# Depthwise 7x7 stage of a fused two-layer kernel: per-channel scalars laid out from diagonals made earlier, and the last step's output interleaved in two halves

## The chip, the cores and the metric

The kernel runs on one core of one Trainium2 chip. A core has the matrix engine TensorE (PE in the profile, its weight loads PEld), VectorE (DVE), ScalarE (ACT) and GpSimd (POOL); SyncE (SP) issues DMA transfers, and so do the queues of ACT and POOL. Each engine executes its own instructions in order; between engines there are semaphores. The metric is the device time of one launch in microseconds, lower is better. Times of a profiled execution are given from the start of its span.

## The reference, cut to what matters

The input is one image of 384 channels, 192 x 192, in fp32. Layer 0 is a group norm, a 1x1 convolution to 1152 channels with 2x2 max pooling, a 3x3 depthwise convolution, channel attention with four top-k softmaxes, a GELU, 2x2 repetition, a projection, and a residual sum. Layer 1 is what the change touches:

```python
def _dwconv(x, w, stride, pad):       # one 7x7 filter for each channel, pad 3
    C = x.shape[1]
    return lax.conv_general_dilated(x, w, window_strides=(stride, stride),
        padding=[(pad, pad), (pad, pad)], dimension_numbers=('NCHW', 'OIHW', 'NCHW'),
        feature_group_count=C)
def _L1_conv_ref(x, weight):
    w_sym = (weight + rot90(weight, 1) + rot90(weight, 2) + rot90(weight, 3)) * 0.25
    return _dwconv(x, w_sym, STRIDE, PAD)
...
x = x + _L1_conv_ref(_gn(x), L1_conv_weight)   # _gn: 32 groups of 12 channels
```

The group norm of layer 1 is `(x - mean) / std` with a mean and a standard deviation for each channel's group, so each channel has three scalars: mean, std and rstd = 1/std.

## The kernel before, in words

The kernel first reads x for the statistics of the first norm, then runs the 1x1 convolution of q and k, the attention, and v with the projection. The sum of layer 0 goes to a DRAM tile `sd` in the layout that the 7x7 stage reads; the banded filter matrices of the 7x7 stage go to `wt` and `wh` in DRAM. This takes up to about 2231 us of the span.

The **7x7 stage** follows. It is a loop of 48 steps, n = 0 to 47, each of CB = 8 channels. For a step, four transfers on ACT's queue load `w` and `h` (filter matrices) and `main` and `aux` (the image, 128 partitions of CP = 4 column strips times TR = 32 rows, and a halo). Each of these has three buffers, and the loads for step n + 2 are issued at the start of step n. Before a step can run, `borders` (POOL, lines 1332 to 1359) writes the mean into the image's border, from `mm` and `mb`; `rest` and `columns` (ACT, lines 1371, 1195, 1196) copy parts of the image and of the filters; and `middle` (DVE, line 1271) adds the residual, std times a permuted identity `eye`, to the middle of the filter matrices, from `sb`.

A step handles its channels in four pairs, q = 0 to 3. For a pair, `sums` makes one PSUM tile `pc` of two banks: for each channel three matmuls (line 1419), two on `main` with `w`, one on `aux` with `h`; an fp32 matmul is two passes in the profile. The tile is then scaled by rstd (from `rb`) into `apart`, in four pieces of 32 partitions: on DVE for q = 0 and 2 (line 1439), on ACT for q = 1 and 3 (line 1437). After q = 1 the loop runs `middle`, `rest` and `columns` of the next step. The pool `pc` has four buffers; the tiles `al` below come from it too.

`apart` holds the four columns of a strip group apart from each other. `spread` (POOL, line 1381) interleaves them into `res` with two copies of 128 x 1152, and SP issues four transfers of 288 KB of it to the output (line 1385), one for each 32 partitions. `spread` of step n - 1 is called in step n behind `borders` of step n + 1, and for step 47 after the loop. `res` has two buffers, `apart` three.

The scalars `mb`, `sb`, `rb` and `mm` lie along the free dimension, 384 channels wide, equal on all partitions. They are made in three tiles of 128 channels. `along` does it: DVE scales the identity by the scalar of each partition into a diagonal `al_dg` (line 1283), PE multiplies ones by it into an `al` tile (line 1284), and DVE copies the tile out (line 1285); `masked` (DVE, line 1289) then makes `mm` of `mb`. The first tile is made ahead of the loop. The other two, kt = 1 and 2, are made at the end of steps 2 and 3:

```python
            if 1 < n < KT + 1:
                done = [along(d, v, n - 1) for d, v in ((mb, mean1), (sb, std1), (rb, rstd1))]
                for d in done:
                    d()
                masked(n - 1)
```

The calls in `keep(...)` stay in the order of the program on their engine, so for this stage the order of the text is the order of each queue.

Of the kernel before, what the change touches and what calls it, by code (L numbers as in the profile page):

```python
# [8 lines left out]
F32 = mybir.dt.float32  # L9
# [4 lines left out]
P = 128  # L14
C = 384
KT = C // P
# [35 lines left out]
TR = 32  # L52
NT = HW // TR
CP = 4
NJ = HW // CP
# [23 lines left out]
def conv_preact_d2(  # L79
# [17 lines left out]
    nc = tc.nc  # L97
# [16 lines left out]
    ident = const.tile([P, P], F32, name="ident")  # L114
    make_identity(nc, ident)
    ones = const.tile([P, P], F32, name="ones")
# [62 lines left out]
    def over_groups(pool, src, n, name):  # L179

        ps = pool.tile([P, KT, n], F32, name=name)
        for jt in range(KT):
            kts = [kt for kt in range(KT) if abs(jt - kt) < 2]
            for kt in kts:
                nc.tensor.matmul(
                    ps[:, jt, :],
                    gsel[:, kt, jt * P : (jt + 1) * P],
                    src[:, kt, :],
                    start=(kt == kts[0]),
                    stop=(kt == kts[-1]),  # L190
                )
        return ps
# [7 lines left out]
    def about(mv, mid, name):  # L200

        d = const.tile([P, KT, 2], F32, name=f"about_{name}")
        nc.vector.tensor_tensor(d[:, :, 0], mv[:, :, 0], mid, ALU.subtract)
        nc.vector.tensor_tensor(d[:, :, 1], d[:, :, 0], d[:, :, 0], ALU.mult)
        nc.vector.tensor_tensor(d[:, :, 1], d[:, :, 1], mv[:, :, 1], ALU.add)
        return d
# [82 lines left out]
    keep = tc.keep_in_program_order  # L289
    with tc.tile_pool(name="stp", bufs=1) as stp, tc.tile_pool(name="xsp", bufs=5) as xsp:  # L290
# [29 lines left out]
        def total(name, n, terms):  # L320

            ps = ptr.tile([P, C], F32, name=name, tag="tr")
            for i, (lhs, rhs) in enumerate(terms):
                keep(
                    nc.tensor.matmul(
                        ps[:, 0:n], lhs, rhs, start=(i == 0), stop=(i == len(terms) - 1)
                    )
                )
            return ps[:, 0:n]

        def sel(kt, jt):
            return gsel[:, kt, jt * P : (jt + 1) * P]
# [15 lines left out]
        def both(kt, most, mid):  # L348

            last = moments(aggregate(kt, 0, NX, "last"), mid, f"{kt}_last")  # L350
            nc.vector.scalar_tensor_tensor(most, last, NX / NB, most, ALU.mult, ALU.add)
            return most
# [20 lines left out]
        for b in reversed(range(NB)):  # L373
            if b == NX - 1:
# [7 lines left out]
                for k, i in ((0, 0), (1, 1), (KT, 2)):  # L382
                    ps = total(f"gs_mid0_{k}", 1, terms[i])
# [54 lines left out]
        kt = TWO  # L438
        mid = mids[:, kt : kt + 1]
        for b in [*range(NB - 2, NX, -2), NX, *reversed(range(NX))]:  # L440
            n = 2 if b > NX else 1
            if b == NX - 1:
                most = aggregate(kt, NX, NB, "most")
                ps = total(
                    "gs_mid0_2", 1,
                    [(sel(1, 2), means[1]), (shared[:, P:], me), (whole, most[:, 0:1])],
                )
# [12 lines left out]
        d = both(kt, dm, mid)  # L460
        ps = total("gs0_2", 2, [(sel(1, 2), ds[1]), (shared[:, P:], de), (whole, d)])
# [89 lines left out]
    with ExitStack() as bx:  # L551
# [55 lines left out]
        with tc.issue_after(loaded):  # L607
            for kt in range(KT):
                cs = slice(kt * P, (kt + 1) * P)
# [535 lines left out]
    with ExitStack() as ex_:  # L1145
# [5 lines left out]
        wide = ex_.enter_context(tc.tile_pool(name="wide", bufs=1))  # L1151
# [5 lines left out]
        outp = ex_.enter_context(tc.tile_pool(name="outp", bufs=2))  # L1157
# [7 lines left out]
        steps = C // CB  # L1165
# [25 lines left out]
        def columns(n):  # L1191

            k = 2 * TR
            w, h = ws[n]
            keep(nc.scalar.copy(h[0:TR, :, 0 : 2 * TR], w[k : k + TR, :, 6 * TR :]))
            keep(nc.scalar.copy(h[REST:P, :, 0:TR], w[k : k + TR, :, 7 * TR :]))
# [46 lines left out]
        mean1 = const.tile([P, KT], F32, name="mean1")  # L1243
        rstd1 = const.tile([P, KT], F32, name="rstd1")
# [6 lines left out]
        with tc.tile_pool(name="gps1", bufs=1, space=PSUM) as gps:  # L1251
            ps = over_groups(gps, mid1.unsqueeze(2), 1, "gs_mid1")
# [3 lines left out]
            ps = over_groups(gps, about(mv1, gmid, "1"), 2, "gs1")  # L1256
            norm_of(ps, gmid, mean1, rstd1, "1")
        std1 = const.tile([P, KT], F32, name="std1")
        mb, sb, rb = [wide.tile([P, C], F32, name=name) for name in ("mb", "sb", "rb")]
        mm = wide.tile([P, C, 5], F32, name="mm")  # L1260

        def tiled(kt):
            return slice(kt * P, (kt + 1) * P)
# [12 lines left out]

        pc = ex_.enter_context(tc.tile_pool(name="pc", bufs=4, space=PSUM))

        def along(dst, src, kt):

            ps = pc.tile([P, 2, 512], F32, name=f"al{kt}", tag="pc")
            dg = wide.tile([P, P], F32, name=f"al_dg{kt}", tag="al_dg", bufs=3)
            keep(nc.vector.tensor_scalar_mul(dg, ident, src[:, kt : kt + 1]))
            keep(nc.tensor.matmul(ps[:, 0, 0:P], ones, dg, start=True, stop=True))
            return lambda: keep(nc.vector.tensor_copy(dst[:, tiled(kt)], ps[:, 0, 0:P]))

        def masked(kt):
            keep(
                nc.vector.tensor_tensor(
                    mm[:, tiled(kt), :],  # L1290
                    mb[:, tiled(kt)].unsqueeze(2).to_broadcast([P, P, 5]),
                    mask.unsqueeze(1).to_broadcast([P, P, 5]),
                    ALU.mult,
                )
            )
# [78 lines left out]
                )  # L1374
            )

        def spread(n, apart):

            res = outp.tile([P, 2, NT * NJ, CP], F32, name=f"res{n}", tag="res")
            for k in range(2):  # L1380
                keep(nc.gpsimd.tensor_copy(res[:, k], apart[:, :, k].rearrange("p e n -> p n e")))  # L1381
            for q in range(CP):
                c = n * CB + 2 * q
                keep(
                    nc.sync.dma_start(
                        out[c : c + 2].rearrange("c (t r) w -> r (c t) w", t=NT),
                        res[q * TR : (q + 1) * TR].rearrange("p c (t j) e -> p (c t) (j e)", t=NT),
                    )
                )

        columns(0)
        borders(0)
        rest(0)
        last = None
        for n in range(steps):
            if n + 2 < steps:
                ws[n + 2] = load_w(n + 2), load_h(n + 2)
                mains[n + 2] = load_main(n + 2), load_aux(n + 2)
            if n + 1 < steps:
                borders(n + 1)  # L1400
            if last is not None:
                spread(n - 1, last)
            (w, h), (main, aux) = ws.pop(n), mains.pop(n)
            apart = outp.tile([P, CP, 2, NT * NJ], F32, name=f"apart{n}", tag="apart", bufs=3)
            ahead = {}

            def sums(q, steps):

                if q not in ahead:
                    ahead[q] = pc.tile([P, 2, 512], F32, name=f"pc{n}_{q}", tag="pc")  # L1410
                for k in range(2):
                    i = 2 * q + k
                    for j in steps:
                        lhs, rhs = (
                            (w[:, i, j * P : (j + 1) * P], main[:, i, :, j : j + NJ]) if j < 2
                            else (h[:, i], aux[:, i, :, 0:NJ])
                        )
                        keep(
                            nc.tensor.matmul(  # L1419
                                ahead[q][:, k, 0 : NT * NJ], lhs, rhs,  # L1420
                                start=(j == 0), stop=(j == 2), skip_group_check=True,
                            )
                        )
                return ahead[q]

            if n == 0:
                for q in range(2):
                    sums(q, range(2))
            for q in range(CP):
                ps = sums(q, range(2 if q in ahead else 0, 3))  # L1430
                c = n * CB + 2 * q
                for g in range(CP):
                    src = ps[g * TR : (g + 1) * TR, :, 0 : NT * NJ]
                    dst = apart[q * TR : (q + 1) * TR, CP - 1 - g]
                    scale = rb[g * TR : (g + 1) * TR, c : c + 1]
                    if q % 2:
                        keep(nc.scalar.mul(dst, src, scale))  # L1437
                    else:
                        keep(nc.vector.tensor_scalar_mul(dst, src, scale))  # L1439
                if q == 1 and n + 1 < steps:  # L1440
                    middle(n + 1)
                    rest(n + 1)
                    columns(n + 1)
            if 1 < n < KT + 1:
                done = [along(d, v, n - 1) for d, v in ((mb, mean1), (sb, std1), (rb, rstd1))]
                for d in done:
                    d()
                masked(n - 1)
            last = apart
        spread(steps - 1, last)  # L1450


# [54 lines left out]
```

## Time and profile before

| | us |
|---|---|
| median of 6 runs | 2829.71 |
| fastest and slowest of them | 2816.27, 2832.23 |
| the profiled execution's own time | 2816.27 |
| its span | 2814.6 |
| PE busy (share of the span) | 2650.7 (94%) |
| DVE, ACT, POOL busy | 2318.0, 870.7, 756.3 |
| matmuls of the 7x7 stage, line 1419: `main` and `aux` | 435.6 and 248.4 |
| evictions of the stage: DVE line 1439, ACT line 1437 | 312.2 and 281.0 |
| `res` copies on POOL, line 1381, 96 of 2275 ns | 215.4 |

The profiled execution is one of the six runs, and the fastest; the difference between its time and its span lies outside the first and last recorded instruction. Busy times of engines overlap, so they are not summed: the share of an engine tells how full it is, and the chain of waits tells which engine's work set the end.

### The profile page before, as it was taken

Reading aid. Unit: us, or ns where it says so; the run is one execution under the profiler, and the core shown is the slowest. Engines: PE = TensorE matmul, PEld = TensorE weight load, DVE = VectorE, ACT = ScalarE, POOL = GpSimd, SP = SyncE. Lnnn points to the kernel's source line nnn. Section 1 sums busy time; section 2 is a strip of 40 time slices with the busy share of each in tenths; the row PEclk is TensorE's granted clock in tenths of the full one; section 3 lists DMA queues with packets and bytes.
Section 4 is the critical chain, followed back from the end, with each engine's and each line's share of the span. In section 5 each row is a group of like instructions: output and inputs, shape, how many; then the busy total and the mean of one; then the engine's idle time right before and its main releaser. Section 6 shows DMA issues by size and latency. Waiting matters only on the chain.

```text
span 2814.6 us, 25628 instructions
## 1 busy us (share of the span) xinstructions
PE 2650.7 (94%) x8717; PEld 1588.4 (56%) x8717; DVE 2318.0 (82%) x3382; ACT 870.7 (31%) x1637; POOL 756.3 (27%) x884
## 2 busy tenths in 40 slices
PE   0399999999999999999999989999999899999997
PEld 0144444444445444444556656666666677777776
DVE  7989887878878878778798878888889778887785
ACT  0141111111111111111202222232323567777775
POOL 1024443100000000000102231010101468878886
PEclk9999999999999999999999999999999999999999
DMA  9966666401001011010335998576674999999997
GB/s 380 403 241 213 228 210 221 154 34 68 34 34 68 34 61 41 34 67 1 104 104 205 327 367 291 171 238 205 203 241 148 338 325 358 370 371 372 374 373 249
DMA packets 234002, 580.98 MB, mean 206 GB/s; under 512 B 16608, under 2 KB 165712, under 8 KB 217104
## 3 DMA queue, kind: packets, MB, share of 16 engines
q1 hardware_dynamic: 173376, 283.44, 28.9%
q0 software_dynamic: 37376, 148.85, 15.5%
q10 hardware_dynamic: 23120, 147.07, 13.9%
q8 instruction: 69, 1.13, 0.2%
q14 instruction: 61, 0.50, 0.1%
HBM read 370.93 MB, written 208.21 MB: 206 GB/s over the span
## 4 chain that ended last, share of the span: by engine, by line
PE 91%; DMA 4%; DVE 4%; ACT 0%; issue 0%; POOL 0%; ACTq 0%; POOLq 0%; SPq 0%; DVEq 0%
PE pq L639 38%; PE pv L537 20%; PE pc L1419 20%; PE pr L985 4%; PE po L961 4%; DMA xs<-in_x_dram 2%; PE grams L709 2%; PE tr L700 2%; PE pq_begun L423 1%; DVE st L318 1%; DMA xv<-in_x_dram 1%; DVE sx L1022 1%; DMA bp<-in_bproj_dram 1%; DMA sd<-sx 0%; DVE apart L1439 0%
## 5 line engine op out<-in xcount | busy, mean ns | idle before, releaser
L639 PE MATMUL pq<-xq,wq 128*128 128x512 f32 x2268 | 990.7, 592 | 0.0
L639 PEld LDWEIGHTS pq<-xq,wq 128*128 128x128 f32 x2268 | 423.0, 190 | 492.2 <-issue 447.7
L682 DVE SCALAR_TENSOR_TENSOR qk<-ring,wd,qk 128x384 f32<-128x384 f32 x1152 | 674.0, 612 | 20.9 <-ACT ring L669 7.1
L537 PE MATMUL pv<-xv,wq 128*128 128x384 f32 x1656 | 543.2, 489 | 10.0 <-DMA xv<-in_x_dram 8.6
L647 DVE TENSOR_REDUCE ring<-pq 128x128 f32<-128x512 f32 x428 | 293.5, 687 | 193.2 <-PE pq L639 192.6
L537 PEld LDWEIGHTS pv<-xv,wq 128*128 128x128 f32 x1656 | 315.5, 191 | 228.8 <-DMA xv<-in_x_dram 6.7
L1419 PE MATMUL pc<-main,w 128*128 128x288 f32 x1536 | 435.6, 406 | 1.1 <-POOL aux L1352 1.1
L1439 DVE TENSOR_SCALAR apart<-pc,rb 32x576 f32<-32x576 f32 x384 | 312.2, 813 | 111.9 <-PE pc L1419 92.0
L1419 PEld LDWEIGHTS pc<-main,w 128*128 128x128 f32 x1536 | 290.4, 189 | 83.9 <-POOL aux L1352 1.3
L1437 ACT ACTIVATE apart<-pc,rb 32x576 f32<-32x576 f32 x384 | 281.0, 732 | 136.2 <-PE pc L1419 131.4
L905 DVE SCALAR_TENSOR_TENSOR vb<-rows,wd,vb 128x576 f32<-128x576 f32 x384 | 313.0, 817 | 11.2
L1419 PE MATMUL pc<-aux,h 128*128 128x288 f32 x768 | 248.4, 405 | 0.0
L691 ACT ACTIVATE junk<-qk 128x384 f32<-128x384 f32 x144 | 75.3, 523 | 543.6 <-DVE qk L682 543.6
L1381 POOL COPY res<-apart 128x1152 f32<-128x1152 f32 x96 | 215.4, 2275 | 65.3 <-DMA out_dram<-res 39.5
L773 POOL TENSOR_TENSOR rn<-rn,halfpos 128x6 f32<-128x6 f32 x1 | 1.4, 1359 | 850.6 <-DVE rn L772 850.6
L1022 DVE TENSOR_TENSOR sx<-xr,y 128x576 f32<-128x576 f32 x180 | 204.0, 1173 | 26.8 <-ACT y L993 21.4
L1063 POOL DMA_DIRECT2D sd<-sx x96 | 72.2, 755 | 505.7 <-DVE sx L1022 486.9
L543 DVE TENSOR_REDUCE rows<-pv 128x192 f32<-128x768 f32 x144 | 137.5, 955 | 66.6 <-PE pv L537 66.5
L1419 PEld LDWEIGHTS pc<-aux,h 128*128 128x128 f32 x768 | 145.4, 189 | 41.6 <-POOL main L1332 0.4
L1042 ACT ACTIVATE wq<-sx,negmid 128x1152 f32<-128x1152 f32 x96 | 120.6, 1256 | 106.8 <-DVE sx L1022 102.7
L985 PE MATMUL pr<-gl,wp 128*128 128x288 f32 x576 | 142.6, 406 | 0.0
L1271 DVE SCALAR_TENSOR_TENSOR w<-eye,sb,w 128x512 f32<-128x512 f32 x96 | 135.3, 1449 | 1.5
(219 smaller groups left out, 2127.5 us busy)
## 6 DMA issues: line engine op xcount, KB each, us to landing
sd<-sx POOLq DMA_DIRECT2D x96, 600.0 KB, 10.3
out_dram<-res SPq DMA_DIRECT2D x192, 288.0 KB, 9.6
main<-sd ACTq DMA_DIRECT2D x46, 1200.0 KB, 5.5
xv<-in_x_dram SPq DMA_DIRECT2D x138, 384.0 KB, 6.9
xr<-in_x_dram SPq DMA_DIRECT2D x45, 1152.0 KB, 12.6
xq<-in_x_dram SPq DMA_DIRECT2D x21, 2304.0 KB, 8.4
w<-wt ACTq DMA_DIRECT2D x46, 1024.0 KB, 6.9
xs<-in_x_dram SPq DMA_DIRECT2D x24, 1536.0 KB, 15.3
```

The costliest lines, as they stand in the source:

```text
L537: nc.tensor.matmul(ps[:, u, 0 : RB * HW], wq[:, kt, o : o + P], xb[:, u, kt, :], start=(kt == 0), stop=(kt == KT - 1),)
L543: nc.vector.tensor_reduce(rows[ct][:, 1 + t0 : 1 + t0 + UT, 1 : PS + 1], ps[:, :, 0 : RB * HW].rearrange("p u (a w b) -> p u w a b", a=2, ...
L639: nc.tensor.matmul(ps, wq[:, kt, ct * P : (ct + 1) * P], rows[:, kt, :, g * 64 : (g + 1) * 64], start=(kt == 0), stop=(kt == KT - 1), skip ...
L647: nc.vector.tensor_reduce(t[:, r0 : r0 + PR, 1 + g * 32 : 1 + (g + 1) * 32], ps.rearrange("p (h a w b) -> p h w a b", h=PR, a=2, b=2), AX. ...
L682: nc.vector.scalar_tensor_tensor(dst, src, w, dst, ALU.mult, ALU.add)
L905: pin(nc.vector.scalar_tensor_tensor(dst, src, w, dst, ALU.mult, ALU.add))
L985: nc.tensor.matmul(ps[:, 0:H], wp[:, ct, ot * P : (ot + 1) * P], gl[:, ct, h * H : (h + 1) * H], start=(ct == 0), stop=(ct == KT - 1),)
L1022: nc.vector.tensor_tensor(bass.AP(flat.tensor, flat.offset + at(e) + a * RUN, [flat.ap[0], [JP, NT], [1, NJ], [at(f) - at(e), 2]],), xq[:, ...
L1381: keep(nc.gpsimd.tensor_copy(res[:, k], apart[:, :, k].rearrange("p e n -> p n e")))
L1419: nc.tensor.matmul(ahead[q][:, k, 0 : NT * NJ], lhs, rhs, start=(j == 0), stop=(j == 2), skip_group_check=True,)
L1437: keep(nc.scalar.mul(dst, src, scale))
L1439: keep(nc.vector.tensor_scalar_mul(dst, src, scale))
```

## The change

`diagonal` is split off from `along`, so that a diagonal can be made at another place than its matmul. In steps n = 2 (for kt = 1) and n = 4 (for kt = 2) the three diagonals are made in the middle of the step, on DVE after `middle` and ahead of the evictions of q = 2. At the end of the step three matmuls write their results side by side into one PSUM tile, three copies take them out, and `masked` follows. Before, kt = 2 was made in step 3, and each of the three had a PSUM tile of its own.

`spread` can do a part of the partitions, with a choice of engine for each of its two copies. In the last step (n = 47) it is called for the partitions of q = 0 and 1 within the step, on POOL as before but for 64 partitions, with the first two output transfers; after the loop it is called for q = 2 and 3, with one copy on DVE and one on ACT, 64 x 1152 each, and the other two transfers. All other steps are as they were.

```diff
+        def diagonal(src, kt):
+            dg = wide.tile([P, P], F32, name=f"al_dg{kt}", tag="al_dg", bufs=3)
+            keep(nc.vector.tensor_scalar_mul(dg, ident, src[:, kt : kt + 1]))
+            return dg
+
         def along(dst, src, kt):
 
             ps = pc.tile([P, 2, 512], F32, name=f"al{kt}", tag="pc")
-            dg = wide.tile([P, P], F32, name=f"al_dg{kt}", tag="al_dg", bufs=3)
-            keep(nc.vector.tensor_scalar_mul(dg, ident, src[:, kt : kt + 1]))
+            dg = diagonal(src, kt)
             keep(nc.tensor.matmul(ps[:, 0, 0:P], ones, dg, start=True, stop=True))
...
-        def spread(n, apart):
-
-            res = outp.tile([P, 2, NT * NJ, CP], F32, name=f"res{n}", tag="res")
-            for k in range(2):
-                keep(nc.gpsimd.tensor_copy(res[:, k], apart[:, :, k].rearrange("p e n -> p n e")))
-            for q in range(CP):
+        def spread(n, apart, res=None, qs=range(CP), copies=None):
+
+            if res is None:
+                res = outp.tile([P, 2, NT * NJ, CP], F32, name=f"res{n}", tag="res")
+            ps = slice(qs[0] * TR, (qs[-1] + 1) * TR)
+            for k, copy in enumerate(copies or [nc.gpsimd.tensor_copy] * 2):
+                keep(copy(res[ps, k], apart[ps, :, k].rearrange("p e n -> p n e")))
+            for q in qs:
...
+            return res
...
+        later = {2 * kt: kt for kt in range(1, KT)}
         for n in range(steps):
...
                     columns(n + 1)
-            if 1 < n < KT + 1:
-                done = [along(d, v, n - 1) for d, v in ((mb, mean1), (sb, std1), (rb, rstd1))]
-                for d in done:
-                    d()
-                masked(n - 1)
+                elif q == 1:
+                    res = spread(n, apart, qs=range(2))
+                if q == 1 and n in later:
+                    dgs = [diagonal(v, later[n]) for v in (mean1, std1, rstd1)]
+            if n in later:
+                ps = pc.tile([P, 2, 512], F32, name=f"al{later[n]}", tag="pc")
+                for i, dg in enumerate(dgs):
+                    cs = slice(i * P, (i + 1) * P)
+                    keep(nc.tensor.matmul(ps[:, 0, cs], ones, dg, start=True, stop=True))
+                for i, d in enumerate((mb, sb, rb)):
+                    keep(nc.vector.tensor_copy(d[:, tiled(later[n])], ps[:, 0, i * P : (i + 1) * P]))
+                masked(later[n])
             last = apart
-        spread(steps - 1, last)
+
+        spread(steps - 1, last, res, range(2, CP), [nc.vector.tensor_copy, nc.scalar.copy])
```

## The prediction, made before the result was known

> **What bounds the kernel now.** I read the share of busy time, then the chain of waits over the two stretches that the diff touches, then windows and the timeline of those stretches.
>
> ```profile
> PE 2650.7 (94%) x8717; PEld 1588.4 (56%) x8717; DVE 2318.0 (82%) x3382; ACT 870.7 (31%) x1637; POOL 756.3 (27%) x884
> PE 91%; DMA 4%; DVE 4%; ACT 0%; issue 0%; POOL 0%; ACTq 0%; POOLq 0%; SPq 0%; DVEq 0%
> ```
> TensorE is the bound: 91% of the chain. So an edit counts only if it shortens a TensorE gap, or what follows its last matmul. The 7x7 stage has 48 steps; an undisturbed one takes 11.64 us (steps 31 and 32 start at 2600.97 and 2612.61). The gaps are at steps 2 and 3. The columns of the next view are window, busy time by engine, clock, DMA share, GB/s:
>
> ```profile
> 2267.00:2271.20 4.20, 1.23 (x7) 1.06 (x7) 3.74 (x6) 3.28 (x5) 3.71 (x5) 0.87 1.06 326
> 2271.20:2274.00 2.80, 2.80 (x9) 2.08 (x8) 1.02 (x2) 0.00 (x0) 2.62 (x4) 0.58 1.00 399
> 2284.20:2286.30 2.10, 0.99 (x6) 0.83 (x7) 1.66 (x6) 2.05 (x4) 0.65 (x2) 1.00 0.43 78
> ```
> PE is nearly empty for 4.2 us after step 2 and 2.1 us after step 3, and after the first gap the clock is 0.58. The timeline says why:
>
> ```profile
> 2264.42 3.31 DVE L1439 TENSOR_SCALAR apart<-pc,rb 32x576 f32<-32x576 f32 x4
> 2267.75 0.28 DVE L1283 TENSOR_SCALAR al_dg<-ident,mean 128x128 f32<-128x128 f32 x1
> 2268.15 2.13 DVE L1283 TENSOR_SCALAR al_dg<-ident,rstd 128x128 f32<-128x128 f32 x1
> 2268.19 0.68 PE L1284 MATMUL al<-al_dg,ones 128*128 128x128 f32 x4 [1.18 <-DVE al_dg L1283]
> 2270.66 0.79 PE L1284 MATMUL al<-al_dg,ones 128*128 128x128 f32 x2 [1.79 <-DVE mb L1285]
> ```
> The matmuls of `along` wait for diagonals that stand on DVE behind the q=2 evictions, and the third for DVE again. The end, as the chain of waits:
>
> ```profile
> 2801.27 0.74 ACT apart L1437
> 2802.01 0.03 POOLq L1381
> 2802.04 0.08 issue
> 2802.12 2.14 POOL res L1381
> 2804.26 2.08 POOLq L1503
> ```
> PE ends at 2799.01, ACT's last eviction at 2802.01, POOL's two copies at 2806.34. Then come four output transfers, with DMA busy from 2807.2 to 2812.9, and the end at 2814.60: 15.6 us after the last matmul.
>
> [...] the rstd diagonal took 2.13 us beside a POOL copy that ended at 2270.20, its neighbour 0.28. [...] clock 0.58 here, matmuls 480 ns apart instead of 243. [...]
>
> **Part 1, the scalars.** The same work for each tile kt=1 and kt=2: three diagonals, three matmuls (six passes), three copies, one `masked`. kt=1 stays at step 2, kt=2 moves from step 3 to step 4. New are the order on DVE (diagonals ahead of the q=2 evictions) and one PSUM tile instead of three.
> What it costs now: step 2 starts at 2255.20, step 4 at 2286.31: 31.11 us, less 2 x 11.64 = 7.83 us lost. Of it 5.54 is at step 2 (start of step 3 4.40 late, then 1.15 for the slow clock: its first pair took 2.60 instead of 1.455), 2.28 at step 3.
> What it will cost at step 2: DVE finishes the two `middle` operations at 2264.38; three diagonals at a pitch of 0.20 (0.28 each, overlapping) put the evictions at 2265.03 instead of 2264.42, and their end at 2268.35. POOL is idle from 2263.16 to 2267.29[...]. PE's six al passes at a pitch of 0.112 take about 0.75 from 2267.01: 2267.76. Then there is a new wait: the pool now gives step 3's first pc the buffer of step 2's q=2, where before it had that of an al tile. So it waits for the last DVE eviction, 2268.4. Queued behind it is all of step 3. Loss 1.55, with a bubble of 0.6 us; step 3's gap of 1.0 us left the clock at 1.00, so I charge no slow clock. Gain 4.0.
> Step 3 loses nothing: gain 2.28. Step 4 gets the al passes, 0.75, and the same wait. There POOL's res copies (2.2 us each) overlap `middle`, which took 1.4 us free and 2.75 to 4.58 beside POOL: the DVE is 0 to 1.6 us late; I take 0.55. Loss 1.3. The three copies (0.29) and `masked` (0.82) follow the evictions on DVE, which idles 0.9 to 3.1 us before the next q=0 ones: hidden. Without that cover they add up to 1.7.
> Sum of part 1: 4.0 + 2.28 − 1.3 = **5.0 us**, between 3.0 and 6.0.
>
> **Part 2, the last step.** Removed from the end: two 128x1152 POOL copies, 4.22 us. Added: in the middle of step 47 two POOL copies of 64 partitions and two transfers; at the end one 64x1152 copy each on DVE and ACT and two transfers.
> The first halves need the q=1 evictions (ACT, 2796.25) and POOL, free at 2795.2. Length: 32x2304 took 2.10 us and 128x1152 2.17, so between half and all of 2.2 each; I take all: done at 2800.6. It decides nothing, since step 46's four transfers, same queue, run until 2801.95; at 1.43 us each (5.70 for four) the two halves run until 2804.8. DVE and POOL overlap only where DVE reads PSUM, and those evictions keep 0.81 us beside POOL.
> The last halves start at 2802.05. ACT: 32x512 takes 0.62, 32x256 0.40, so 0.84 ns an element plus 0.19: 1.15 us. [...] Done at 2803.25. From issue to first packet was 0.84: 2804.1, before the halves ahead are through. So the last two run 2804.8 to 2807.65, and with the 1.7 us from last packet to end the span ends at 2809.35. The DMA becomes the bound of the tail. Gain **5.25 us**; with a 2.2 us DVE copy 4.8; with the queue free at once 5.8 (the last two would run from 2804.1); if step 46's copies and transfers run 2.8 us late, 2.5.
> On SP the two early transfers stand behind step 46's, the last of which is issued at 2798.58, and the late two behind them; nothing else is left in its queue. The buffer that all four use was last read by step 45's transfers, and DMA traffic has a pause from 2793.0 to 2796.0, so they had landed. Behind the last copies nothing is queued on ACT or DVE. POOL's early copies stand behind step 46's (until 2795.2), and POOL has nothing after them.
>
> **Sum.** 5.0 + 5.25 = 10.25 us. Against the profiled execution (span 2814.6, time 2816.27): 2804.4 and 2806.0. That execution was the fastest of six; the median is 13.4 above it, for which no view has a cause. I carry the difference over: 2829.71 − 10.2 = **2819.5 us**. Within 0.3% (8.5 us) a measurement of this kernel can't tell a change from none, so the forecast sits just beyond it.
>
> **Rivals.**
> *A, both gains* (0.62): 2819.5; own range 2818 to 2822 from the bounds.
> *B, the stage's transfers take part 1 back* (0.20). In steps 25 to 43 POOL ends the borders of a step within about 1 us of its start:
>
> ```profile
> 2612.45 0.50 POOL L1359 COPY aux<-mb 30x384 f32<-30x384 f32 x1
> 2612.61 1.13 PE L1419 MATMUL pc<-main,w 128*128 128x288 f32 x4
> ```
> DMA moves 370 GB/s there. If TensorE comes 5 us earlier and the loads don't, it waits. Against: loads are issued when TensorE frees a buffer, and their queue stood empty 5.2, 5.1 and 2.9 us between steps 3 and 7, so they can come forward too. Then only part 2 stays: 2824.5.
> *C, slower* (0.07). As B, but every wait also drops the clock. From a gap above 1 us and below 4.2 us a step on, each costs 1.15 us as at step 2. Twelve such of the 19 tight steps: 13.8 + 5.0 − 10.25 = 8.5 us slower: 2838. Against: PE shows only 0.2 us of waits after step 4.
> *D, the tail doesn't shorten* (0.11), since transfers of one queue are the bound and step 46's run late: part 1 alone and some 0 to 2.5 more, 2822 to 2825.
>
> **Numbers.** 2819.5, range 2813 to 2828: A to B and D, 2818 to 2825, and 3 to 5 us at each side because a median of six that spread over 16 us moves. C is left out. Faster by over 0.3%: nearly all of A, 0.62. Within: B, D and A's edge, 0.31. Slower: C, 0.07.
>
> **What would show it.** Step 3 starts 13.2 us after step 2 (was 16.0) and its first pair takes 1.46; step 4 follows 11.64 later; step 5 follows after 12.4 to 14. Before pc at steps 3 and 5, the releaser is DVE `apart`. After the last matmul the end comes 10.3 us later, not 15.6, with no gap between step 46's transfers and the end's. Wrong if PE shows POOL or DMA waits in steps 25 to 43 (B, C), or if the DMA idles before the last two transfers.

## The result and the profile after

The kernel after takes **2820.29 us** (median of 21 runs, 2810.43 to 2826.45), the kernel before in the same comparison 2827.84 us (43 runs, 2812.46 to 2836.76). The ratio is **0.9973**, 95% interval 0.9963 to 0.9983: 7.6 us faster, with 4.8 to 10.5 inside the interval. A repetition on another chip gave 0.9977 (0.9968 to 0.9986). The forecast was 10.25 us.

The profiled span went from 2814.6 to only 2813.5 us, and by the shares of busy time on the page TensorE is still the fullest engine (the chain of waits on this page breaks off after ACT's last copy and can't be read further):

```profile
PE 2648.8 (94%) x8717; PEld 1587.6 (56%) x8717; DVE 2348.8 (83%) x3383; ACT 873.0 (31%) x1638; POOL 745.0 (26%) x884
```

DVE is 30.8 us busier, and 29.9 of this is `middle` (96 operations, mean 1759 ns, was 1449; 62 of them took over 1 us, was 43). This belongs to the execution and not to the change: a second profile of after, below, has a mean of 1440 ns, and e2, with the scalars as before, 1790. PE isn't longer for it (2648.8 us, before 2650.7).

To read the change, the 7x7 stage has to be cut out of the span, since what lies ahead of it differs between executions: step 0 starts at 2231.61 us in the profile before and at 2238.84 in the profile after, a difference of 7.23 us where no instruction was changed. From step 0 to the end it is 582.96 before, 574.62 after: 8.34 us shorter. The first matmul of each step (line 1428 now) cuts it into parts. "2→3" is from the start of step 2 to that of step 3. The last column, from the last matmul to the end of the span, is called the tail below.

| us | 2→3 | 3→4 | 4→5 | 2→5 | 5→47 | tail |
|---|---|---|---|---|---|---|
| before, profiled | 16.04 | 15.07 | 11.66 | 42.77 | 489.23 | 15.56 |
| after, profiled | 13.32 | 11.72 | 13.82 | 38.85 | 489.57 | 10.80 |
| difference | −2.72 | −3.35 | +2.16 | −3.92 | +0.34 | −4.76 |

The end of step 2 in the timeline of the profile after (columns: start, us, engine and line, operation):

```profile
2271.54 0.27 DVE L1281 TENSOR_SCALAR al_dg<-ident,mean 128x128 f32<-128x128 f32 x1
2271.93 0.27 DVE L1281 TENSOR_SCALAR al_dg<-ident,rstd 128x128 f32<-128x128 f32 x1
2272.24 3.30 DVE L1448 TENSOR_SCALAR apart<-pc,rb 32x576 f32<-32x576 f32 x4
2274.07 0.83 PE L1461 MATMUL al<-al_dg,ones 128*128 128x128 f32 x6
2275.75 1.21 PE L1428 MATMUL pc<-main,w 128*128 128x288 f32 x4 [0.85 <-POOL main L1336]
```

The diagonals come ahead of the q=2 evictions, at 0.27 us each, and the six `al` passes run without a stop. Then PE stands still for 0.85 us. The releaser named, POOL's `main`, had ended at 2275.01. What ends last is the q=2 evictions (DVE, line 1448), at 2275.54; 0.21 us later the first matmul of step 3 starts. The windows of this gap and of what follows show no drop of the clock (columns as in the prediction: window, length, busy time by engine, clock, DMA share, GB/s):

```profile
2274.90:2275.75 0.85, 0.00 (x1) 0.03 (x1) 0.82 (x2) 0.84 (x2) 0.79 (x2) 1.00 1.04 355
2275.75:2278.55 2.80, 2.80 (x12) 2.21 (x13) 2.08 (x4) 1.81 (x3) 2.66 (x3) 1.00 1.08 305
```

The clock was 0.58 after the 4.2 us stretch of before in which PE was busy for 1.23; it is 1.00 here. And the end of the span, in the timeline; the last matmul ends at 2802.66:

```profile
2800.02 4.27 POOL L1387 COPY res<-apart 64x1152 f32<-64x1152 f32 x2 [1.21 <-ACT apart L1446]
2802.70 2.96 ACT L1446 ACTIVATE apart<-pc,rb 32x576 f32<-32x576 f32 x4 [2.79 <-PE pc L1428]
2805.73 2.17 ACT L1387 COPY res<-apart 64x1152 f32<-64x1152 f32 x1
2805.74 1.15 DVE L1387 COPY res<-apart 64x1152 f32<-64x1152 f32 x1 [2.66 <-ACT apart L1446]
```

DVE's copy is through at 2806.89, ACT's only at 2807.90. SP issues the last two transfers from 2807.93. The output queue's packets stop at 2808.14; those of the last two transfers ran from 2808.76 to 2811.78, so it stood still for 0.6 us.

### The profile page after: what moved, and what is told of

It is laid out like the page before. It is cut to its first block, busy times and chain, and to the rows that moved or that the text cites. A ratio compares the mean times of both kernels' runs of the same rounds, so it can differ in the third digit from the quotient of the medians.

```text
span 2813.5 us, 25638 instructions
## 1 busy us (share of the span) xinstructions
PE 2648.8 (94%) x8717; PEld 1587.6 (56%) x8717; DVE 2348.8 (83%) x3383; ACT 873.0 (31%) x1638; POOL 745.0 (26%) x884
## 5 line engine op out<-in xcount | busy, mean ns | idle before, releaser
L639 PEld LDWEIGHTS pq<-xq,wq 128*128 128x128 f32 x2268 | 423.0, 190 | 492.2 <-issue 448.2
L1387 POOL COPY res<-apart 128x1152 f32<-128x1152 f32 (+1 forms) x96 | 220.3, 2319 | 11.6 <-ACT apart L1446 8.7
L1063 POOL DMA_DIRECT2D sd<-sx x96 | 72.2, 755 | 511.7 <-DVE sx L1022 492.2
L1271 DVE SCALAR_TENSOR_TENSOR w<-eye,sb,w 128x512 f32<-128x512 f32 x96 | 165.2, 1759 | 1.5
## 6 DMA issues: line engine op xcount, KB each, us to landing
sd<-sx POOLq DMA_DIRECT2D x96, 600.0 KB, 10.3
```

The costliest lines, as they stand in the source:

```text
L639: nc.tensor.matmul(ps, wq[:, kt, ct * P : (ct + 1) * P], rows[:, kt, :, g * 64 : (g + 1) * 64], start=(kt == 0), stop=(kt == KT - 1), skip ...
L1271: nc.vector.scalar_tensor_tensor(mid, eye.unsqueeze(1).to_broadcast([P, 4, P]), sb[:, c : c + 1], mid, ALU.mult, ALU.add,)
L1387: keep(copy(res[ps, k], apart[ps, :, k].rearrange("p e n -> p n e")))
```

## The experiments

All are edits of one of the two kernels. "Before" and "after" are the kernels above. Times with a ratio were measured against before on the same chip; the others are one execution with its profile, and show stretches, not whether the kernel is faster.

**The two kernels again.** Unchanged.

> The kernel before, a second look. Theory A' (of the 5.5 us that step 2 lost in the first profile, 2.1 us are a chance lock of the rstd diagonal by a POOL copy, and 1.15 the slow clock after it): without that meeting step 2 to step 5 takes about 40.3 us, as in the kernel with the tail alone; with it 42.8 us. Rival: 42.8 us whenever the whole change is absent, and the tail-only kernel differs by something else.

> The changed kernel, a second look. Diagonals stand where POOL copies only delay the operations ahead of them: step 2 to step 5 38.9 to 39.4 us again; last matmul to end 10.8 us; steps 5 to 47 between 489.2 and 491.8 us, since short waits for POOL and DMA fall there by chance.

| us | 2→3 | 3→4 | 4→5 | 2→5 | 5→47 | tail |
|---|---|---|---|---|---|---|
| before again | 14.56 | 14.03 | 11.64 | 40.23 | 492.29 | 15.59 |
| after again | 13.32 | 11.71 | 13.32 | 38.35 | 489.07 | 10.76 |

After repeats. Before does not: step 2→3 is 1.48 us shorter than in its first profile, and step 3→4 1.04. Its timeline shows why:

```profile
2254.73 0.70 DVE L1283 TENSOR_SCALAR al_dg<-ident,mean 128x128 f32<-128x128 f32 x1
2255.35 0.27 DVE L1283 TENSOR_SCALAR al_dg<-ident,std 128x128 f32<-128x128 f32 x1
2255.55 0.46 DVE L1283 TENSOR_SCALAR al_dg<-ident,rstd 128x128 f32<-128x128 f32 x1
2255.58 0.68 PE L1284 MATMUL al<-al_dg,ones 128*128 128x128 f32 x4 [1.59 <-DVE al_dg L1283]
```

The third diagonal took 0.46 us here, not 2.13, and step 3's first four matmuls 1.15, not 2.13. So the diagonal of 2.13 us is not there in every execution of this kernel. In the first profile the third diagonal began 0.16 us after a copy of POOL (line 1344, 2267.99 to 2270.20) and ended 0.08 us after it. Such a diagonal, of 2.1 us beside a POOL copy, is what the expectation above calls a lock; it is called a long diagonal below, and what makes it long was not shown.

**One part at a time.** e1 has the scalars of after and the end of before; e2 the reverse.

```diff
 e1: - elif q == 1: res = spread(n, apart, qs=range(2))
     - spread(steps - 1, last, res, range(2, CP), [nc.vector.tensor_copy, nc.scalar.copy])
     + spread(steps - 1, last)
 e2: the block at the end of the step as in the kernel before (along, 1 < n < KT + 1)
```

> Only the scalars' half of the change; the last step as before. In the trace, step 2 starts to step 5 starts: 38.9 us as in the changed kernel (42.8 before); last matmul to end 15.6 us as before (10.8 in the changed kernel). Time: theory A (the two halves add, each as its stretch of the trace shows) 3.9 us under before. Rival B (the stage's transfers take this half back): steps 5 to 47 longer by as much, PE waits for POOL or DMA there, time as before.

> Only the last step's half of the change; scalars as before. Theory A: step 2 to step 5 again 42.8 us with the slow clock after step 2 (first pair of step 3 2.6 us); last matmul to end 10.8 us; time 4.8 us under before. Rival D (step 46's transfers run late where the front of the stage is not shortened): last matmul to end over 12.5 us.

e1: ratio 0.9985 (0.9977 to 0.9993), which is 4.2 us of 2805.6; steps 2→5 39.38 us, tail 15.56. e2: 0.9984 (0.9976 to 0.9993), 4.5 us; steps 2→5 40.27 where 42.8 was expected, tail 10.80. Each profile has the part it should have, and not the other. The timed gains add up to 8.7 us, beside 7.6 for the whole change; the intervals allow both. The tail's 4.76 us is found again in full. For the scalars, e2 is one more execution with the old order and without the long diagonal, and it agrees with "before again" (40.23). Against these two, the new order with one tile gains 0.9 to 1.9 us (39.38 and 38.35), not 3.9.

**Three PSUM tiles in place of one** (the diagonals stay ahead).

```diff
-                ps = pc.tile([P, 2, 512], F32, name=f"al{later[n]}", tag="pc")
...
+                    ps = pc.tile([P, 2, 512], F32, name=f"al{later[n]}_{i}", tag="pc")
+                    keep(nc.tensor.matmul(ps[:, 0, 0:P], ones, dg, start=True, stop=True))
```

> The changed kernel, but with three PSUM tiles for the three scalars as before; diagonals ahead. If the diagonals' place does it all, step 2 to step 5 is 38.9 us as with one tile. If the tiles matter: the second al tile takes the buffer of q=2 and waits for its evictions, the third for the copy of the first, and step n+1 for the copy of the second, so each of the two groups costs about 0.6 us more (two copies of 0.29 at a pitch of 0.2, a matmul of 0.25 between): 40.1 us.

Steps 2→5 took 40.06 us: step 2→3 14.13, 4→5 14.22. The timeline:

```profile
2252.88 3.30 DVE L1448 TENSOR_SCALAR apart<-pc,rb 32x576 f32<-32x576 f32 x4
2256.33 0.72 PE L1461 MATMUL al<-al_dg,ones 128*128 128x128 f32 x4 [1.21 <-DVE apart L1448]
2256.83 0.29 DVE L1464 COPY sb<-al 128x128 f32<-128x128 f32 x1 [0.32 <-PE al L1461]
2257.22 1.21 PE L1428 MATMUL pc<-main,w 128*128 128x288 f32 x4 [0.17 <-issue]
```

Now the second and third `al` tiles wait for the evictions (until 2256.18), and step 3 for the copy that empties a tile. Step 3 starts 1.03 us after the evictions in place of 0.21. So the single tile is worth 0.82 us at each of the two places, and the diagonals ahead, without it, gain little against the old order without the long diagonal (40.06 beside 40.23 and 40.27). No run kept kt = 2 in step 3, so what its move to step 4 is worth by itself is not known.

**The diagonals at their old place** (one tile stays).

```diff
-                if q == 1 and n in later:
-                    dgs = [diagonal(v, later[n]) for v in (mean1, std1, rstd1)]
             if n in later:
+                dgs = [diagonal(v, later[n]) for v in (mean1, std1, rstd1)]
```

> The changed kernel with one PSUM tile, but with the diagonals made at the end of the step, behind the q=2 evictions. If one tile does it all: 38.9 us from step 2 to step 5. If the diagonals' place matters: the evictions end 0.7 us earlier, then the diagonals take 0.7 us (up to 2.7 if one meets a POOL copy), then the six al passes 0.75: each group costs about 2.2 us (0.5 more than the 1.7 of the changed kernel), up to 4.2[...]: 40 to 44 us.

Step 2→3 was 16.25 us, 3→4 12.57, 4→5 13.89: 42.71 for 2→5, as in the first profile of before. The long diagonal was there again, now that of the mean:

```profile
2258.53 2.10 POOL L1348 COPY aux<-main 32x2304 f32<-32x2304 f32 x1
2258.58 2.13 DVE L1281 TENSOR_SCALAR al_dg<-ident,mean 128x128 f32<-128x128 f32 x1
2260.86 1.62 PE L1460 MATMUL al<-al_dg,ones 128*128 128x128 f32 x6 [3.03 <-DVE al_dg L1281]
2262.27 2.06 PE L1428 MATMUL pc<-main,w 128*128 128x288 f32 x4
```

DVE's diagonal began 0.05 us after POOL's copy and ended 0.08 us after it, as in the first profile of before (0.16 and 0.08). The matmuls were slow again too: the six `al` passes behind the wait of 3.03 us took 1.62 us, where they take 0.83 in after, step 3's first four matmuls 2.06, where they take 1.21 in after, and step 3→4 was 12.57 us in place of 11.72.

Of the four executions with late diagonals (before twice, e2, e4) two had a long one. Of the seven with the diagonals ahead of the q=2 evictions (after three times, e1, e3, e6, e7) none had: in after's first profile, e1 and e6 each diagonal took 0.27 to 0.29 us. (e8 below, with the diagonals late in an earlier step, had one of 2.13 us too, but nothing waited for it.)

So the diagonals ahead take away an accident of some 2.5 us (42.77 − 40.23), seen in two of four executions, too few to give its frequency. They also gain a little without it: in step 4 e4 had no long diagonal, and step 5 came 13.89 us after step 4, beside 13.32 in after again, where `middle` took as long (2.76 and 2.74 us).

**No extra tile at all.** e5 puts the scalars into unused columns of the q=3 tile `pc` of steps 2, 4 and 6 (two matmuls each), takes them out on ACT, and makes the diagonals a step earlier. It takes away the suspected wait on the evictions by taking away the tile.

```diff
+                if q == CP - 1 and n in later:
+                    ahead[q] = pc.tile([P, 2, 512], F32, name=f"pc{n}_{q}", tag="pc")
+                    for k, dg in enumerate(dgs):
+                        keep(nc.tensor.matmul(ahead[q][:, k, SIDE], ones, dg, start=True, stop=True, ...))
...
+                for k, (d, _, kt) in enumerate(later[n]):
+                    keep(nc.scalar.copy(d[:, tiled(kt)], ps[:, k, SIDE]))
```

> The changed kernel, but the scalars' matmuls write the unused columns of the q=3 tile ahead of its own matmuls (mean and std of kt=1 in step 2, of kt=2 in step 4, rstd of both in step 6), from diagonals made at the end of the step before; ScalarE copies them out after its q=3 evictions. Theory A (what is left of the loss is the wait of step n+1 for the late q=2 evictions): no such wait, only the four passes of three groups, 0.45 to 0.6 us each: step 2 to step 7 59.6 to 60.1 us (62.2 in the changed kernel, 58.2 with no loss). Rival (the loss is the matmuls and the weight loads themselves): about as in the changed kernel, 62 us.

Step 2→3 and 4→5 took 12.09 us each, 2→5 35.81, 2→7 60.32 (after 62.21). The timeline, around the start of step 3 at 2260.20:

```profile
2256.85 0.61 PE L1448 MATMUL pc<-al_dg,ones 128*128 128x128 f32 x4
2257.32 3.30 DVE L1464 TENSOR_SCALAR apart<-pc,rb 32x576 f32<-32x576 f32 x4
2259.72 0.65 PE L1433 MATMUL pc<-aux,h 128*128 128x288 f32 x2
2260.20 0.65 PE L1433 MATMUL pc<-main,w 128*128 128x288 f32 x2
```

The q=2 evictions still end at 2260.62, and PE starts step 3 before that, with no pause. So the wait of after is the one on these evictions, by way of the buffers of `pc`.

In the six profiles with one extra tile and early diagonals (after three times, e1, e6, e7 below: twelve steps) the next step starts 0.21 us after the evictions' end in every case, though their end moves between 12.97 and 13.90 us after the start of the step, with the length of `middle` (2.69 to 3.53 us for its two operations). e5's one execution was as long as one of before (2801.49 and 2801.83): steps 0→2 took 26.93 us, where all other profiles have 23.5 to 25.1 (POOL waited 4.61 us for a load of `main` there), and the tail was 11.87.

**Which side of the copy is strided.** The last copies read `apart` with a stride and write `res` in order. e6 turns the order of elements round.

```diff
-                keep(copy(res[ps, k], apart[ps, :, k].rearrange("p e n -> p n e")))
+                keep(copy(res[ps, k].rearrange("p n e -> p e n"), apart[ps, :, k]))
```

> The changed kernel, but every interleaving copy walks the other way: contiguous reads of 288 and writes with a stride of four, instead of strided reads and contiguous writes. If the strided read is what makes POOL and ScalarE take 1.88 ns an element (2.17 us for 1152) where contiguous copies take 0.92: ScalarE's last copy 1.2 us, POOL's copies 1.1 us each, last matmul to end 10.2 us (the transfers' queue allows no more than 0.6 us). If a stride on either side costs the same: all as in the changed kernel.

Groups by line and shape (mean ns after the comma), e6:

```profile
L1387 POOL COPY res<-apart 128x1152 f32<-128x1152 f32 x94 | 218.9, 2406 | 11.0 <-ACT apart L1446 8.1
L1387 POOL COPY res<-apart 64x1152 f32<-64x1152 f32 x2 | 4.3, 2230 | 1.1 <-ACT apart L1446 1.1
L1387 ACT COPY res<-apart 64x1152 f32<-64x1152 f32 x1 | 2.2, 2245 | 0.1
L1387 DVE COPY res<-apart 64x1152 f32<-64x1152 f32 x1 | 1.2, 1199 | 2.7 <-ACT apart L1446 2.7
```

After has 2323, 2161, 2172 and 1151 ns in these rows. A stride on the write side costs no less than one on the read side: the idea that reading was the trouble fell. Both forms cost ACT and POOL about 1.9 ns an element (2172 / 1152), twice what copies of 32x2304 without such an order take (ACT 2120 ns, POOL 2102 ns, or 0.92 and 0.91 an element), and DVE 1.0. No run has a copy of 64x1152 without a stride on either side.

**The last copies divided.** ACT's copy is the longer of the two last copies, so e7 gives a third of its elements to DVE. After was timed once more beside it.

```diff
+                (nc.vector.tensor_copy, 0, slice(0, NT * NJ)),
+                (nc.scalar.copy, 1, slice(cut, NT * NJ)),      # cut = NT * NJ // 3
+                (nc.vector.tensor_copy, 1, slice(0, cut)),
```

> The kernel after, unchanged, as the partner of the two that follow. Own theory: against the kernel before 0.9973 to 0.9985 (4 to 7.6 us), that is 4.75 us from the last step and 1.4 to 1.9 from the scalars in an execution without the 2.13 us diagonal, less what steps 5 to 47 vary by. Rival: the scalars are worth the 5 us of the prediction in every execution: 0.9965.

> The kernel after, with the last copy of the second half (1152 elements, 2.17 us on ScalarE) divided: VectorE takes the first half's copy (1.15 us) and then a third of the second (0.4), ScalarE two thirds (1.45). Theory, that ScalarE's copy at 1.88 ns an element holds the end: both copies end 1.55 us after they begin in place of 2.17, the last two transfers follow directly on the queue's earlier ones (ended 0.6 us before), and the tail after the last matmul goes from 10.80 to 10.2. Rival, that the DMA queue sets the end: 10.8, with the gap ahead of the last two transfers kept or moved.

After: 0.9977 (0.9968 to 0.9986), tail 10.80 in its profile, steps 2→5 38.93. e7: 0.9966 (0.9957 to 0.9976), 1.8 us less by the medians, within the intervals. Its profile can't decide between the theories, since another wait came up (tail 11.90):

```profile
2784.34 4.23 POOL L1388 COPY res<-apart 64x1152 f32<-64x1152 f32 x2 [3.00 <-DMA out_dram<-res]
2788.01 1.56 ACT L1388 COPY res<-apart 64x768 f32<-64x768 f32 x1
2788.02 1.97 DVE L1388 COPY res<-apart 64x1152 f32<-64x1152 f32 x2 [2.66 <-ACT apart L1447]
```

POOL's copies of step 47 waited 3.00 us for the buffer `res`, which step 45's output transfers still read. Then the transfers of the first half are late, and the queue holds the end. The same wait stands in e4 (3.00 us, tail 12.62) and e5 (2.95, 11.87), so in three of the nine profiles in which the first half uses the shared `res`; it occurred in none of the three of after. In these three runs POOL had waited for `res` between steps 5 and 46 too, 30 to 38 us in total; in after, its third run, e2 and e6 it never did. In after again it had (36.9 us), and yet `res` was free at the end. It is the prediction's case of "step 46's copies and transfers run 2.8 us late".

**All together.** e8 joins e5's columns, a buffer of its own for the last `res`, step 46 also written in two halves, the first half of step 47 copied by POOL and ACT side by side, two of the last four evictions given to DVE, and e7's division. e9 is e8 without the halves of step 46 and without the divided evictions.

```diff
 e8: + res tag "res_end", bufs=1, for n == steps - 1
     + copies=[(nc.gpsimd.tensor_copy, 0, every), (nc.scalar.copy, 1, every)]   # first half of step 47
     + if n == steps - 2: half = spread(n, apart, qs=range(2))                  # not in e9
     + if q % 2 and not (n == steps - 1 and q == CP - 1 and g >= 2):            # not in e9
```

> The other tiles' scalars in unused columns of the step's own q=3 PSUM tile, as in the side-columns run, and a shorter last step: step 46's first half is also written early, the first half of step 47 is copied by GpSimd and ScalarE side by side, the last four evictions are shared by ScalarE and VectorE, the last copies are divided two to one, and the last result has a buffer of its own. Theory: steps 2 to 7 take 60.3 us as there; the last copies begin 0.9 us sooner (two evictions of 0.74 and 0.82 instead of four) and take 1.55, the queue is free by then, so the tail is 9.2 to 9.6. Sum against the kernel after: 1.4 + 1.4 = 2.8 us, ratio to the kernel before 0.9963 to 0.9975. Rival: what the front gives is returned in the long run, by waits for loads or GpSimd: then only the tail's 1.4 us is seen, and steps 5 to 47 take over 492.

> The side-columns kernel with a shorter end: step 46 stays whole on GpSimd (as in the kernel after), the evictions stay as they were, the last result has its own buffer, the first half of step 47 is copied by GpSimd and ScalarE side by side (2.2 us in place of 4.27), and the last copies are divided two to one (1.6 us in place of 2.17). Theory, that ScalarE's last copy sets the end once the queue is free early: copies begin 3.05 us after the last matmul, end at 4.65, and the two last transfers follow at once: tail 10.2. Rival, that the queue of output transfers holds the end whatever the copies do: 10.5 or more, as in the run before this one, with the two last transfers joined to earlier ones without a gap. Steps 2 to 5: 35.8 again. Ratio to the kernel before 0.996 to 0.9975.

e8 (5 runs): 0.9960 (0.9946 to 0.9973), steps 2→5 35.81, 2→7 60.83, tail 10.49 where 9.2 to 9.6 was expected. The sign of its rival, steps 5→47 over 492 us, came too (492.89); by the medians it is still 5.5 us faster than after, more than the 2.8 of the theory. Its evictions did not run side by side:

```profile
2783.36 1.66 DVE L1466 TENSOR_SCALAR apart<-pc,rb 32x576 f32<-32x576 f32 x2 [1.11 <-ACT apart L1464]
2785.05 1.62 DVE L1389 COPY res<-apart 64x1152 f32<-64x1152 f32 x2
2785.10 1.60 ACT L1389 COPY res<-apart 64x768 f32<-64x768 f32 x1 [1.78 <-DVE apart L1466]
```

DVE waited for ACT's two (until 2783.32), so that the copies began as late as ever. And POOL, with copies of 64 partitions that last nearly as long as those of 128 (2185 and 2282 ns), was busy without a break until 2783.77; the output queue then ran without a gap to the end.

e9 (5 runs): **0.9959** (0.9945 to 0.9973), 2791.8 us beside 2804.73; steps 2→5 35.81, 2→7 59.97, tail 10.25 where 10.2 was expected:

```profile
2778.66 2.22 ACT L1389 COPY res<-apart 64x1152 f32<-64x1152 f32 x1
2778.69 2.19 POOL L1389 COPY res<-apart 64x1152 f32<-64x1152 f32 x1 [1.15 <-ACT apart L1464]
2784.41 1.61 ACT L1389 COPY res<-apart 64x768 f32<-64x768 f32 x1
2784.41 1.63 DVE L1389 COPY res<-apart 64x1152 f32<-64x1152 f32 x2 [2.60 <-ACT apart L1464]
```

From the issue of the last two transfers to the end it is 5.5 us in after (2807.93 to 2813.45) and 5.5 in e9 (2786.10 to 2791.64), although the queue had a gap in the one and none in the other. So ACT's copy set the end of after, and a shorter one, with the first half written earlier, brings the end forward by as much: the copy is 0.56 shorter, the tail 0.55. The transfers now follow each other without a gap, so the queue is next in line. e9 is the fastest version measured; its interval overlaps that of after.

## Why the prediction was right, and where it was off

The side and the order of size were right, and the predicted 2819.5 us is 0.8 from the measured median. That closeness is partly luck: the gain was forecast 2.65 us too large (10.25, measured 7.6), and the base, the median of six runs, stood 1.87 above the median of the 43 runs of before in the comparison. The prediction gave 0.62 to a gain of over 0.3%. The measured 0.27% is below that line and its interval, 0.17% to 0.37%, lies on both sides of it, so that part stays undecided. (Its 0.31 for a gain within 0.3% is B and D alone; nothing was left for A's edge, where the measurement fell.)

**Part 2, the end: mechanism right, one term mis-sized.** Predicted 10.3 us from the last matmul to the end, measured 10.80, 10.76 and 10.80. The term is "ACT: 32x512 takes 0.62, 32x256 0.40 … 1.15 us". Those rows are copies without a stride; the one at the end has a stride, and it took 2.17. A warning was in reach: 128x1152 in the same strided order on POOL stood in the page at 2275 ns. For DVE's copy the prediction had no row of the trace to go by; it took 1.15 us, 1.00 ns an element, and ended 1.01 us before ACT's, so it did not set the end. By ACT's 2.17 us, "The DMA becomes the bound of the tail" was wrong: its own test, that the DMA idles before the last two transfers, came out (0.6 us), and e9 shows that ACT's copy was the bound. The two are close: in after again the last four transfers ran without a gap, and the tail was 10.76 all the same. POOL's copies of 64 partitions took all of 2.1 us each, as chosen. The bad case of that part, transfers of an earlier step still in `res`, is real: the tail of 12.62 us in e4 leaves a gain of 2.9. The prediction's argument that step 45's transfers had landed was read from one profile, and held in six of nine.

**Part 1, the scalars: steps right, the base a chance.** Against the profile that the prediction was made from, 3.92 us came of the 5.0, inside 3.0 to 6.0. The steps: step 3 started after 13.32 us (13.2 predicted) and its first pair was not slow (the first four matmuls took 1.21 us, in before 2.13); step 4 followed after 11.72 (11.64 predicted); step 5 after 13.82 (12.95 taken, 12.4 to 14 allowed). So what is missing is mostly at step 5 (0.87 of it): a longer `middle` made the evictions later than the 0.55 charged, and the wait passes that on in full. The new wait on the q=2 evictions was there in each profile with the single tile and the diagonals ahead, and e5 shows it is what holds PE.

The step that failed is the first, what the scalars cost now: "Of it 5.54 is at step 2 (start of step 3 4.40 late, then 1.15 for the slow clock". That loss held the long diagonal (2.13 us) and the slow clock after it (0.58), and both were carried over to every run. Without the long diagonal, as in "before again", step 2 loses 14.56 − 11.64 = 2.92 us and step 3 2.39; part 1 is then worth 40.23 − 38.35 = 1.9 us, or 0.9 to 1.9 over the executions of after and e1. If the long diagonal comes in some of the executions, as in two of the four seen, the mean lies between that and 3.9. The timed 4.2 us of e1 has an interval from 2.0 to 6.5, which holds such a mean, and the 5.0 of the prediction too.

**Rival B** (the stage's transfers take part 1 back) isn't seen in after. Steps 5→47 took 489.1 to 492.7 us in the six profiles with the scalars in one tile (after three times, e1, e6, e7), and 489.2 to 492.3 in three with the scalars as before (before twice, e2): the same spread. What makes it are short waits at a few steps; the view of PE's waits of "before again", from step 5 to step 46 (us in total, times, longest), has these:

```profile
PE pc L1419 <- POOL aux L1359: 2.1, 4, 0.9
```

In the third run of after, seven steps lasted 11.84 to 12.57 us in place of 11.64, together 3.7. So POOL's borders come late by some tenths of a microsecond with either order of the scalars. Behind POOL there can be a load: before one of these waits POOL itself had waited 0.87 us for `main`. What decides in a given execution whether they come was not found; nor was what shifts the start of the stage from 2215.6 to 2238.8 us. e5, e8 and e9 took 492.2 to 492.9, of which 0.8 to 1.7 us are in steps 5 and 6, where they put more scalars.

**Rival C** (each wait drops the clock) is refuted for single waits of the lengths seen. In after PE stopped for 0.85 and 1.35 us ahead of steps 3 and 5, and the clock was 1.00 in the 1.2 us behind each stop. Behind stops of 1.21 us (e3) and 1.59 (before again), ahead of `al` matmuls, the next step's first four matmuls took 1.21 and 1.15 us, against 1.21 in after. The slow matmuls shown stood behind the two long diagonals in PE's way: in before at a clock of 0.58, behind a stretch of 4.2 us of which PE was still busy for 1.23, and in e4 behind 3.03 us without a matmul. How long a wait has to be for that was not shown.

**Rival D** (the tail does not shorten) is refuted: the tail fell by 4.7 us or more in each profile where `res` was free. Its cause, transfers that run late, did come in three of nine profiles, and left 2.9 to 3.7 us of the gain.

## What to carry to other kernels

Before a duration goes into a sum, look whether its neighbours of the same row have it too: an operation that took eight times its siblings' time (2.13 us beside 0.28) may be an event of that execution, and removing it is worth its frequency times its length, so profile the kernel a second time. Price a copy by a row with the same engine and the same access order, not only the same element count: in one strided order ACT and POOL took 1.9 ns an element, DVE 1.0. And where a tile is added to a pool in rotation, ask which earlier reader the next user will inherit: a wait that is gone for one engine came back as one for another, and of the versions tried only the use of spare columns of a tile that is there anyway removed it.

## What the runs showed that was not expected

- An interleaving fp32 copy cost ACT 2172 ns for 64x1152 and POOL 2161, about 1.9 ns an element, whether the stride was on the read or the write side; DVE took 1151 ns. ACT's copy of 32x2304 without one takes 0.92 ns an element.
- POOL's copy took 2.13 to 2.21 us on 64 partitions and on 128 alike at the end of the span.
- DVE's last copy took 1.15 us in after but 1.56 in e5 and 2.42 in e4, where POOL's copies were still running when it began (at 2791.00 and 2793.64, POOL's until 2791.55 and 2794.93; ACT's beside it took 2.17 and 2.32). This looks like the long diagonals, but no run separates the cause.
- The time from the issue of the last two transfers to the end was 5.5 us with a queue that was empty before them and with one that was just running out.
